# Chunked last stores, a chained transform, epsilon and a middle tap moved between engines

## The chip, the core and the metric

The kernel runs on one core of a Trainium2 chip. Its engines work at the same time, each through its own queue in order: TensorE (PE in the profile, its weight loads PEld) for matrix products into PSUM, VectorE (DVE) and ScalarE (ACT) for elementwise work, GpSimd (POOL) for small arithmetic and for starting transfers, SyncE (SP) only for starting transfers. Sixteen DMA engines move data between HBM and the on-chip SBUF, whichever queue a transfer was started from. The metric is the device time of one execution in microseconds.

## The reference

The input x is 4 batches x 512 times x 128 frequencies x 64 channels in float32; D = 128 x 64 = 8192. Two layers follow each other, all in float32.

Layer 0, per batch:

- attention part: a layer norm over D (epsilon 1e-5), three projections D to 64 (k, v, r), a decayed running sum of k*v over time, times sigmoid(r), projected back to D and added to x;
- frequency convolution: layer norm over D, a 3-tap convolution along frequency that mixes the 64 channels, gelu, added to x;
- time convolution: layer norm over D, then for every one of the D columns its own causal 3-tap filter along time,

```python
xt = jnp.swapaxes(xn, 1, 2)
to = lax.conv_general_dilated(xt, time_W, (1,), [(KS - 1, 0)], ..., feature_group_count=d)
to = to + time_b[None, :, None]
to = layernorm(jnp.swapaxes(to, 1, 2), time_ln_g, time_ln_b)
x = x + to.reshape(b, t, f, h)
```

- feed-forward: 64 to 256, gelu, 256 to 64, added to x.

Layer 1: a moving average over 25 times (ends repeated) is the trend; x minus the trend goes through a real Fourier transform over time, of which 128 modes are kept; each channel's modes are mixed by a complex 128x128 matrix; the inverse transform is added to the trend.

## The kernel before

**Layer 0** holds x column-major: 64 chunks of 128 columns x 512 times per batch, worked on in 32 pairs (tiles of 128x1024). Its stages per batch are project (the projections; J), scan (Z), attend_and_convolve (attention's output and the frequency convolution; A), convolve_time (C), open_feed (O) and feed_forward (F). TensorE's order is written out by hand: `in_turn` runs two generators side by side and takes instructions from each by given shares. The pairs that matter here are C of batch 0 beside A of batch 1, C of 1 beside A of 2, C of 2 beside A of 3, and later C of 3 beside F of 2. The queues of the other engines are ordered by the framework's planner, from its own estimates of durations and from priorities that follow the program; `keep_in_program_order` and `issue_after` tie single instructions.

One step of the time convolution handles one pair of chunks. `normed` loads x2 and normalises it on VectorE (a multiplication at L642 and a subtraction at L645, rows rb and mb broadcast over the pair). `tapped` then, per chunk, takes the last tap and the bias on ScalarE (L650, written to `to`) and adds the middle and first tap with one `scalar_tensor_tensor` each on VectorE (L654, on 511 and 510 elements); GpSimd corrects the first two times (L660) and stores the pair to DRAM (L661). ScalarE squares `to` (L701), and two steps later TensorE adds up sums and squares (`add_up`, L252). For batches 1 and 2, 14 of the 32 pairs are done ahead of time, inside the feed-forward of the batch before (`convolve_ahead`, which calls `tapped` itself); `convolve_time` does the other 18 and squares the 14 that it loads again (buffers with the tag "mid", four of them, which feed_forward uses too). Batches 0 and 3 do all 32 there.

In the same stretch of time, one step of attend_and_convolve costs VectorE three operations on 128x1024: x = a + xp (L540), which frees TensorE's PSUM pair "a", z = x * rb (L544), and, after ScalarE's gelu (L592), x2 = gelu + x (L594), which `add_up` needs.

The four layer norms of each batch end in `rsqrt` (L232): GpSimd adds epsilon (L233) and raises to -1/2 (L234); then TensorE spreads the result over rows (`spread`, L242).

**Layer 1** handles two batches at a time, twice: `transform`, `mix`, `invert`, with 16 slabs of 512 columns per batch. In `transform`, `butterflies` loads two slabs (SP), forms v = first half minus second half and u = their sum for each (L1019), and sum and difference of the two u (ev, L1026); `products` multiplies them (L1041 on v, L1055 on ev, L1064 for the ends) and copies to the spectrum xf. `butterflies` is a generator: the first pair of the second half is drawn piece by piece from within `invert` of the first half. Within one pair the operations are tied one behind the other; from one pair to the next they are not. `mix` goes through 16 groups of four channels: `differ` forms d = real minus imaginary (L1104, VectorE, two buffers), `common` multiplies d (L1110) into one of two PSUM pairs and copies it out on ScalarE (L1116, L1117), `second_turn` copies the remaining part on VectorE (L1152), `own` multiplies the rest (L1123), `join` adds (L1159). `invert` goes through 32 slabs: inverse waves (L1202, L1212), the moving average from the slab's own four chunks of times (L1249) and from halos of 12 neighbouring times (L1256), four additions on VectorE (L1261) and one store of 1 MB by GpSimd (L1264). The last slab of each half takes its four PSUM banks from the two pairs "a", since the next transform's first products take the others.

Of the kernel before, what the change touches and what calls it, by code (L numbers as in the profile page):

```python
# [10 lines left out]
F32 = mybir.dt.float32  # L11
# [69 lines left out]
def layer0(ctx, tc, dram, x, xt, vecs, wkvr, wo, wdec, wconv, fbias, w1, fb1, w2, fb2, x4):  # L81
# [150 lines left out]
    def rsqrt(rs, var):  # L232
        nc.gpsimd.tensor_scalar(rs, var, EPS, None, ALU.add)  # L233
        nc.gpsimd.tensor_tensor(rs, rs, mhalf, ALU.pow)  # L234

# [36 lines left out]
    def moments(mean, square, tag):  # L272

        var, rs, mrs = cols(f"var{tag}"), cols(f"rs{tag}"), cols(f"mrs{tag}")
        nc.vector.tensor_tensor(var, mean, mean, ALU.mult)
        nc.vector.tensor_tensor(var, square, var, ALU.subtract)
        rsqrt(rs, var)
        nc.vector.tensor_tensor(mrs, mean, rs, ALU.mult)
        return rs, mrs
# [146 lines left out]
    def scan(b):  # L426
# [10 lines left out]
        nc.vector.tensor_tensor(sq, sq, mv[:, :, 1], ALU.add)  # L437
        nc.vector.tensor_copy(var, mv[:, :, 1])
        rsqrt(rs, var)
# [206 lines left out]

    def tapped(b, i, xr, to, pinned=False):
        for j in range(2):
            c = slice(2 * i + j, 2 * i + j + 1)
            nc.scalar.activation(  # L650
                to[:, j, :], xr[:, j, :], AF.Identity, bias=tb_all[:, c], scale=vec[:, W2, c]
            )
            for k, w in ((1, W1), (2, W0)):
                tap = nc.vector.scalar_tensor_tensor(  # L654
                    to[:, j, k:], xr[:, j, : SL - k], vec[:, w, c], to[:, j, k:], ALU.mult, ALU.add
                )
                if pinned and j == 0 and k == 1:
                    tc.keep_in_program_order(tap)
        cc = slice(2 * i, 2 * i + 2)
        nc.gpsimd.tensor_tensor(to[:, :, 0:2], to[:, :, 0:2], fix[:, cc, :], ALU.add)  # L660
        nc.gpsimd.dma_start(tod[b][cc].rearrange("c p t -> p c t"), to)  # L661
# [13 lines left out]
    def convolve_time(b):  # L675
# [10 lines left out]
        for k in range(n + 2):  # L686
# [3 lines left out]
            if k < n:  # L690
# [8 lines left out]
                normed(b, made + k, x2, xr, rb, mb, made > 0 and k < 4)  # L699
                tapped(b, made + k, xr, to)  # L700
                nc.scalar.activation(sq, to, AF.Square)  # L701
# [215 lines left out]
def layer1(ctx, tc, x4, wri, dftv, dftu, dftd, dfte, idfte, idfto, avg, avgh, out, after):  # L917
# [36 lines left out]
    def pair():  # L954
        return ps.tile([P, 2, SL], F32, tag="a", name="a", bufs=2)
# [33 lines left out]
    def behind(b, n, ins):  # L989

        return tc.issue_after(ins) if b == 0 and n < 5 else nullcontext()

    def butterflies(b0, n):

# [3 lines left out]
        us, vs, ts = [], [], []  # L998
        made = None
        two = 1 if g == NS // 4 else 2  # L1000
# [5 lines left out]
        for i, xin in enumerate(xins):  # L1006
# [10 lines left out]
            for uv, op in ((v, ALU.subtract), (u, ALU.add)):  # L1017
                with tc.issue_after(made.ins) if made else behind(b, at, after["vector"]):
                    made = nc.vector.tensor_tensor(uv.rearrange("p k n -> p (k n)"), xin[:, 0, :], xin[:, 1, :], op)  # L1019
                if op == ALU.subtract or i == 0:  # L1020
                    yield made
        for op in (ALU.add, ALU.subtract):
            t = io.tile([P, 2, SL], F32, tag="ev", name="ev")
            t_, u0, u1 = (x[:, 0:two, :].rearrange("p k n -> p (k n)") for x in (t, *us))
            with tc.issue_after(made.ins):
                made = nc.vector.tensor_tensor(t_, u0, u1, op)  # L1026
            ts.append(t)
# [56 lines left out]
    def mix(xf, last):  # L1084
# [89 lines left out]
        for g in range(1, NG):  # L1174
# [5 lines left out]
            if g + 2 < NG:  # L1180
                with tc.issue_after(turned[g].ins):
                    differ(g + 2)
# [11 lines left out]
    def invert(b0, xf, ahead):  # L1194
# [33 lines left out]
        def fetch(n):  # L1228
# [11 lines left out]
            blocks[n] = xin, halo, []  # L1240

        def within(n, js):
            xin, _, po = blocks[n]
            if n == G * NS - 1:
                po += [whole[:, k, :] for whole in (pair(), pair()) for k in range(2)]
            for j in js:
                if n < G * NS - 1:
                    po.append(bank())
                nc.tensor.matmul(po[j], lhsT=avg_sb[:, j, :], rhs=xin[:, j, :], start=True, stop=False)  # L1249

        def across(n):
            b, s = divmod(n, NS)
            xin, halo, po = blocks.pop(n)
            for j in range(NT):
                at = slice(32 * j, 32 * j + (HALO if j in (0, NT - 1) else 2 * HALO))
                nc.tensor.matmul(po[j], lhsT=avgh_sb[at, :], rhs=halo[at, :], start=False, stop=True)  # L1256
            pm = halves.pop(n)
            begun = None
            for j in (1, 3, 0, 2):
                with tc.issue_after(begun.ins) if begun else nullcontext():  # L1260
                    nc.vector.tensor_tensor(by_n(xin[:, j, :]), by_n(po[j]), by_c(pm[j % 2][:, j // 2, :]), ALU.add)  # L1261
                if j == 3 and n == G * NS - 1:
                    begun = next(ahead)
            nc.gpsimd.dma_start(  # L1264
                out[b0 + b, :, s * SL : (s + 1) * SL].rearrange("(c p) d -> p c d", p=P), xin
            )

# [17 lines left out]
    with tc.manual_schedule(engines={nc.tensor.engine}):  # L1285
        ahead = butterflies(0, 0)
        for b0 in range(0, B, G):
            xf = spec.tile([P, 2, H, G, NF // 2, 2], F32, tag="xf", name="xf")
            last = transform(b0, xf, ahead)
            ahead = butterflies(b0 + G, 0) if b0 + G < B else iter([None] * 4)  # L1290
            mix(xf, last)
            invert(b0, xf, ahead)
# [105 lines left out]
```

## Time and profile before

| | |
|---|---|
| Median of three runs | 3612.3 us (3609.67 to 3617.32) |
| Profiled execution: time, span | 3609.67 us, 3607.9 us |
| Mean granted TensorE clock | 0.986 |
| Busy: PE, VectorE, ScalarE, GpSimd | 3418.7, 2803.8, 1933.0, 505.1 us |
| DMA | 894 MB, mean 248 GB/s |

The span runs from the first instruction to the last; the time has 1.8 us around it. In the rows of the profile, L12 is line 12 of the kernel before; a row of the timeline gives the start, the time taken, the engine, the line, the output and input tiles, and in brackets the idle time before it with what ended it. Matmuls overlap, so a busy TensorE is not one at its peak. The stages lie roughly so in the span: projection of batch 0 to 245 us, the three pairs C beside A at about 508 to 770, 1190 to 1390 and 1835 to 2020 with feed-forwards between and behind them, layer 1 from 2687, its second half from 3137.

### The profile page before, as it was taken

The numbers are of one execution on the slowest core, as the hardware profiler recorded it, in microseconds if no ns is written. First come the engines' busy times: TensorE is split into PE (matmuls) and PEld (weight loads), VectorE is DVE, ScalarE is ACT, GpSimd is POOL, SyncE is SP. The second block draws the span as 40 slices with busy tenths as digits, with TensorE's granted clock in tenths as the row PEclk, the third lists the DMA queues.
The fourth block names the chain that finished last, engine by engine and source line by source line (L and its number), as shares of the span: only waits on it lengthen the run. The fifth ranks groups of instructions, "written<-read, shape, count | busy, mean of one in ns | idle before, by whom it ended". The sixth has DMA issues, their size and how long they took to land. (4 is left out here: it accounts for less than half of the span.)

```text
span 3607.9 us, 56794 instructions
## 1 busy us (share of the span) xinstructions
PE 3418.7 (95%) x21689; PEld 1279.1 (35%) x21689; DVE 2803.8 (78%) x3524; ACT 1933.0 (54%) x2451; POOL 505.1 (14%) x657
## 2 busy tenths in 40 slices
PE   8999998889998899999999989999999999999998
PEld 3433332234333223443322333334332533325433
DVE  4576779976776896677789799956669788897887
ACT  0023456655666565666656588878877810177200
POOL 0000012210101211011112121110000401004011
PEclk9999999999999999999999999999999999999999
DMA  9886657787885788788568777755659378993687
GB/s 311 294 288 229 219 201 258 253 280 268 285 282 183 252 278 279 271 294 289 180 230 283 238 239 261 247 182 200 221 180 294 102 246 293 309 290 106 230 300 266
DMA packets 410478, 894.00 MB, mean 248 GB/s; under 512 B 31840, under 2 KB 82784, under 8 KB 410208
## 3 DMA queue, kind: packets, MB, share of 16 engines
q1 hardware_dynamic: 336640, 620.46, 52.8%
q0 software_dynamic: 71680, 268.46, 20.5%
q8 instruction: 173, 2.83, 0.3%
q10 hardware_dynamic: 1888, 1.45, 0.1%
q14 instruction: 97, 0.79, 0.1%
HBM read 621.74 MB, written 268.50 MB: 247 GB/s over the span
## 5 line engine op out<-in xcount | busy, mean ns | idle before, releaser
L778 PE MATMUL p<-mid,w_sb 64*64 64x512 f32 x2048 | 550.8, 596 | 17.7 <-DVE wx L791 17.6
L778 PE MATMUL pb<-mid,w_sb 64*64 64x512 f32 x2048 | 533.8, 596 | 0.0
L768 ACT ACTIVATE mid<-m,fb_sb 128x1024 f32<-128x1024 f32 x256 | 284.9, 1113 | 92.1 <-PE m L763 90.9
L768 ACT ACTIVATE mid<-c,fb_sb 128x1024 f32<-128x1024 f32 x256 | 284.6, 1112 | 92.5 <-PE c L763 90.3
L763 PE MATMUL c<-x,w_sb 64*64 64x512 f32 x2016 | 278.4, 606 | 13.0 <-ACT mid L768 6.6
L763 PE MATMUL m<-x,w_sb 64*64 64x512 f32 x2016 | 283.2, 613 | 7.4 <-ACT ob L812 5.4
L1218 ACT COPY two<-a 128x512 f32<-128x512 f32 x64 | 37.5, 586 | 428.2 <-PE a L1202 414.0
L778 PEld LDWEIGHTS p<-mid,w_sb 64*64 64x64 f32 x2048 | 153.9, 135 | 292.7 <-issue 263.1
L413 PE MATMUL a<-xp,wx 128*128 128x512 f32 x512 | 235.2, 603 | 0.5 <-DVE me L269 0.5
L1249 PE MATMUL b<-xin,avg_sb 128*128 128x512 f32 x496 | 223.3, 592 | 0.0
L599 ACT ACTIVATE sq<-x 128x1024 f32<-128x1024 f32 x128 | 135.0, 1055 | 159.4 <-DVE x L594 159.3
L1261 DVE TENSOR_TENSOR xin<-b,pm 128x512 f32<-128x512 f32 x248 | 153.9, 683 | 83.7 <-PE b L1256 73.9
L252 PE MATMUL st<-x,ones 128*32 128x512 f32 x512 | 185.5, 609 | 25.5 <-DVE x L594 25.5
L654 DVE SCALAR_TENSOR_TENSOR to<-kd,vec,to 128x511 f32<-128x511 f32 (+1 forms) x272 | 196.9, 743 | 10.5 <-ACT to L650 8.1
L731 ACT ACTIVATE kd<-kd,vec 128x512 f32<-128x512 f32 x256 | 192.7, 803 | 3.1 <-DVE kd L723 3.1
L540 DVE TENSOR_TENSOR x<-a,xp 128x1024 f32<-128x1024 f32 x128 | 156.1, 1219 | 38.8 <-PE a L536 36.4
L734 DVE TENSOR_TENSOR x<-kd,kx 128x1024 f32<-128x1024 f32 x126 | 154.0, 1222 | 33.5 <-ACT kd L731 33.5
L654 DVE SCALAR_TENSOR_TENSOR z<-x,vec,z 128x511 f32<-128x511 f32 x240 | 175.6, 744 | 5.4 <-ACT z L650 2.3
L791 DVE SCALAR_TENSOR_TENSOR x4t<-p,fb_sb,x 128x512 f32<-128x512 f32 x64 | 47.7, 746 | 159.6 <-PE pb L778 157.1
L536 PE MATMUL a<-rst,wo_sb 64*64 64x512 f32 x1024 | 143.5, 628 | 27.7 <-DVE x L540 25.5
L597 POOL DMA_DIRECT2D x<-x x128 | 93.3, 729 | 531.3 <-DVE x L594 497.2
L722 DVE TENSOR_TENSOR kd<-kh,rm 128x1024 f32<-128x1024 f32 x128 | 155.7, 1219 | 7.1 <-ACT rm L286 4.6
(292 smaller groups left out, 6855.4 us busy)
## 6 DMA issues: line engine op xcount, KB each, us to landing
xp<-in_xt SPq DMA_DIRECT2D x256, 512.0 KB
xin<-x SPq DMA_DIRECT2D x96, 1024.0 KB
kh<-to SPq DMA_DIRECT2D x156, 512.0 KB
x<-x POOLq DMA_DIRECT2D x128, 512.0 KB, 4.3
kx<-x SPq DMA_DIRECT2D x128, 512.0 KB
x<-ob POOLq DMA_DIRECT2D x64, 1024.0 KB, 7.9
out<-xin POOLq DMA_DIRECT2D x64, 1024.0 KB, 7.3
x<-x SPq DMA_DIRECT2D x96, 512.0 KB
```

The source lines that it names most:

```text
L252: nc.tensor.matmul(st[32 * q : 32 * q + 32, :], lhsT=ones, rhs=src[:, j, :], start=first, stop=last,)
L413: nc.tensor.matmul(pa[:, k, :], lhsT=wq[:, j, k * P : (k + 1) * P], rhs=xp[:, j, :], start=first and j == 0, stop=last and j == 1,)
L540: nc.vector.tensor_tensor(x1, at, xp, ALU.add)
L654: tap = nc.vector.scalar_tensor_tensor(to[:, j, k:], xr[:, j, : SL - k], vec[:, w, c], to[:, j, k:], ALU.mult, ALU.add)
L722: nc.vector.tensor_tensor(d, to, pair_of(rb), ALU.mult)
L731: tc.keep_in_program_order(nc.scalar.activation(d[:, j, :], d[:, j, :], AF.Identity, bias=vec[:, B4, c], scale=vec[:, G4, c]))
L734: nc.vector.tensor_tensor(x3, d, x2, ALU.add)
L763: nc.tensor.matmul(pm[halves[j], h, :], lhsT=w1_sb[halves[h], q * H : (q + 1) * H], rhs=x3[halves[h], j, :], start=True, stop=True,)
L768: gelu = nc.scalar.activation(mid, pm, AF.Gelu_apprx_tanh, bias=fb1_sb[:, q : q + 1])
L778: nc.tensor.matmul(sums2[i][j][halves[h], :], lhsT=w2_sb[halves[j], q, :], rhs=mid[halves[j], h, :], start=q == 0, stop=q == 3,)
L1249: nc.tensor.matmul(po[j], lhsT=avg_sb[:, j, :], rhs=xin[:, j, :], start=True, stop=False)
L1261: nc.vector.tensor_tensor(by_n(xin[:, j, :]), by_n(po[j]), by_c(pm[j % 2][:, j // 2, :]), ALU.add)
```

## The change

It has five parts.

1. `rsqrt`: epsilon is no longer added by GpSimd. In `moments` the subtraction that forms the variance becomes one `scalar_tensor_tensor` that adds epsilon too; in `scan` the copy of the variance becomes a `tensor_scalar` that adds it. GpSimd keeps the power.
2. `tapped` takes an optional tile `mid`. With it, ScalarE also multiplies each chunk by the middle tap (two more activations), VectorE's two middle taps are left out, and one VectorE addition over both chunks adds `mid`, shifted by one time, to `to`. `convolve_time` passes such a tile for batches 0, 1 and 2, from the buffers "mid".
3. `butterflies` ties each pair of a transform behind the pair before it on VectorE.
4. In `mix`, d of group 3 is no longer tied behind the first `second_turn`.
5. The last two slabs of the whole kernel are stored by chunks of 256 KB, each behind its own addition, from the SP and ScalarE queues in turn instead of 1 MB from GpSimd. For the very last slab TensorE takes the halo products first and then the own chunks in the order in which the additions follow.

```diff
     def rsqrt(rs, var):
-        nc.gpsimd.tensor_scalar(rs, var, EPS, None, ALU.add)
-        nc.gpsimd.tensor_tensor(rs, rs, mhalf, ALU.pow)
+        nc.gpsimd.tensor_tensor(rs, var, mhalf, ALU.pow)
...
-        nc.vector.tensor_tensor(var, square, var, ALU.subtract)
+        nc.vector.scalar_tensor_tensor(var, square, EPS, var, ALU.add, ALU.subtract)
...
-        nc.vector.tensor_copy(var, mv[:, :, 1])
+        nc.vector.tensor_scalar(var, mv[:, :, 1], EPS, None, ALU.add)
...
+            if mid is not None:
+                nc.scalar.activation(mid[:, j, :], xr[:, j, :], AF.Copy, scale=vec[:, W1, c])
             for k, w in ((1, W1), (2, W0)):
+                if mid is not None and k == 1:
+                    continue
                 tap = nc.vector.scalar_tensor_tensor(
...
+        if mid is not None:
+            nc.vector.tensor_tensor(to[:, :, 1:], to[:, :, 1:], mid[:, :, : SL - 1], ALU.add)
...
-                tapped(b, made + k, xr, to)
+                mid = bk.tile([P, 2, SL], F32, tag="mid", name="mid", bufs=4) if b < B - 1 else None
+                tapped(b, made + k, xr, to, mid=mid)
...
+    behind_pair = [None]
...
-        made = None
+        made = behind_pair[0]
...
-                with tc.issue_after(made.ins) if made else behind(b, at, after["vector"]):
+                with behind(b, at, after["vector"]), tc.issue_after(made.ins) if made else nullcontext():
...
-                made = nc.vector.tensor_tensor(t_, u0, u1, op)
+                made = behind_pair[0] = nc.vector.tensor_tensor(t_, u0, u1, op)
...
-                with tc.issue_after(turned[g].ins):
+                with tc.issue_after(turned[g].ins) if g > 1 else nullcontext():
                     differ(g + 2)
...
+        def final(n):
+            return b0 + G == B and n == G * NS - 1
+
         def within(n, js):
...
+            if final(n):
+                edges(n, True)
+                js = (1, 3, 0, 2)
             for j in js:
...
-                nc.tensor.matmul(po[j], lhsT=avg_sb[:, j, :], rhs=xin[:, j, :], start=True, stop=False)
+                nc.tensor.matmul(po[j], lhsT=avg_sb[:, j, :], rhs=xin[:, j, :], start=not final(n), stop=final(n))
+
+        def edges(n, start):
+            _, halo, po = blocks[n]
+            for j in range(NT):
+                at = slice(32 * j, 32 * j + (HALO if j in (0, NT - 1) else 2 * HALO))
+                nc.tensor.matmul(po[j], lhsT=avgh_sb[at, :], rhs=halo[at, :], start=start, stop=not start)
...
+                if b0 + G == B and n > G * NS - 3:
+                    queue = nc.sync if j % 2 else nc.scalar
+                    queue.dma_start(out[b0 + b, j * P : (j + 1) * P, c], xin[:, j, :])
+            if b0 + G == B and n > G * NS - 3:
+                return
...
             last = transform(b0, xf, ahead)
+            behind_pair[0] = None
```

More of the change, by code (lines that the diff above doesn't have):

```diff
@@ L645, in normed, with tapped @@
         nc.vector.tensor_tensor(xr, xr, pair_of(mb), ALU.subtract)
-    def tapped(b, i, xr, to, pinned=False):
+    def tapped(b, i, xr, to, pinned=False, mid=None):
         for j in range(2):
@@ L1248, in within @@
                     po.append(bank())
-                nc.tensor.matmul(po[j], lhsT=avg_sb[:, j, :], rhs=xin[:, j, :], start=True, stop=False)
+                nc.tensor.matmul(po[j], lhsT=avg_sb[:, j, :], rhs=xin[:, j, :], start=not final(n), stop=final(n))
[4 more added lines that the diff above has]
+                nc.tensor.matmul(po[j], lhsT=avgh_sb[at, :], rhs=halo[at, :], start=start, stop=not start)
         def across(n):
             b, s = divmod(n, NS)
[L1253 to L1256, printed above, removed]
+            c = slice(s * SL, (s + 1) * SL)
+            if not final(n):
+                edges(n, False)
+            xin, _, po = blocks.pop(n)
             pm = halves.pop(n)
@@ L1263, in across @@
                     begun = next(ahead)
-            nc.gpsimd.dma_start(
-                out[b0 + b, :, s * SL : (s + 1) * SL].rearrange("(c p) d -> p c d", p=P), xin
-            )
+                if b0 + G == B and n > G * NS - 3:
[3 more added lines that the diff above has]
+                return
+            nc.gpsimd.dma_start(out[b0 + b, :, c].rearrange("(c p) d -> p c d", p=P), xin)
         fetch(0)
```

## The prediction, made before the changed kernel was run

> **What bounds the kernel now.** I read the page's busy shares first, then the busy time by stretch, then what TensorE waited for, and then the timeline at the places that the change touches.
>
> ```profile
> span 3607.9 us, 56794 instructions
> PE 3418.7 (95%) x21689; PEld 1279.1 (35%) x21689; DVE 2803.8 (78%) x3524; ACT 1933.0 (54%) x2451; POOL 505.1 (14%) x657
> ```
>
> TensorE is the bound over the whole, but a mean hides the stages. The busy time by stretch (length, then busy us of PE, PEld, DVE, ACT, POOL, the clock, DMA share and GB/s):
>
> ```profile
> 545.00:765.00 220.00, 192.58 (x1076) 49.42 (x1076) 218.00 (x242) 133.98 (x184) 59.12 (x80) 0.99 0.78 258
> 1230.00:1400.00 170.00, 158.89 (x1004) 45.14 (x996) 156.01 (x158) 107.53 (x147) 35.64 (x53) 1.00 0.83 282
> ...
> 3152.00:3245.00 93.00, 92.72 (x632) 23.94 (x624) 86.74 (x77) 69.48 (x117) 0.00 (x0) 1.00 1.03 294
> ```
>
> The first stretch is the time convolution of batch 0 beside the attention of batch 1: VectorE is busy 218 of 220 us, TensorE only 88%. There VectorE's work is the time. The second, the same pair of stages for batches 1 and 2, is mixed: TensorE 93%, VectorE 92%. The third is the second transform of layer 1, where the DMA engines are full (1.03). What TensorE waited for, in the rows that the change bears on (total us, times, longest):
>
> ```profile
> PE a L242 <- POOL rs L234: 8.5, 5, 3.4
> PE b L1055 <- DVE ev L1026: 7.0, 3, 5.6
> ...
> PE a L1110 <- DVE d L1104: 5.1, 2, 2.6
> PE p L242 <- POOL rs L234: 4.2, 2, 2.1
> ```
>
> **The middle tap on ScalarE.** Each of 68 steps (32 for batch 0, 18 each for batches 1 and 2, whose other 14 were made ahead by code that passes no mid) loses two VectorE taps and gains one addition over both columns. VectorE's timeline in the first stretch has the price of each, by distance from start to start:
>
> ```profile
> 597.86 1.21 DVE L645 TENSOR_TENSOR kd<-kd,rm 128x1024 f32<-128x1024 f32 x1
> 599.00 1.21 DVE L540 TENSOR_TENSOR x<-a,xp 128x1024 f32<-128x1024 f32 x1
> 600.13 0.73 DVE L654 SCALAR_TENSOR_TENSOR to<-kd,vec,to 128x511 f32<-128x511 f32 x1
> 600.79 1.21 DVE L544 TENSOR_TENSOR z<-x,rm 128x1024 f32<-128x1024 f32 x1
> ```
>
> A tap takes 0.66 us of the engine's time, a two-input operation on 1024 elements 1.13. So a step saves 2 x 0.66 - 1.13 = 0.19 us: 6.1 us in batch 0, 3.4 us each in batches 1 and 2, 12.9 us at most. ScalarE pays two multiplications of 128x512 per step. No row shows exactly this one; it lies between the copy at L1218 without a column operand (0.59 us) and the activation at L650 with two (0.80 us, 0.71 from start to start). I take 0.70, near L650, which reads the same tile. 64 of them are 45 us in batch 0's stage of about 32 x 8.3 = 266 us; ScalarE goes from 61% to 78% there and still has room.
>
> The skill speaks against this edit: the Trainium skill, "ScalarE: Activation LUTs", Rules for kernel authors, wants multiplications on VectorE, not ScalarE. Its timing (What ACT_TABLE_LOAD costs) would give an estimate of 0.71 us for a 512-element activation with one column operand, 1.42 us of ScalarE for 0.19 us of VectorE. By the rule the edit loses; by the rows above it trades idle time for busy time.
>
> In batch 0 I take 5.5 of the 6.1 us: VectorE's list of waits from 560 to 760 is empty, and TensorE needs only 88% of the time. What is queued behind the new wait: the addition needs the second multiplication, and VectorE takes its queue in order, so an addition placed too early holds up the attention's x and z, for which TensorE waits at L536 and L252. In batches 1 and 2 the engines take turns at being late: in 1240 to 1420 VectorE waited 4.3 us in 9 places for ScalarE's to at L650 and 13.3 us for its gelu at L592, both now behind more ScalarE work. I put the two at -0.5 us together, between -6.8 and, if each multiplication delays a gelu by a quarter of itself (36 steps x 2 x 0.18), +13.
>
> **Epsilon on VectorE.** The two VectorE instructions are exchanged for others of the same 128x4 size (0.16 us rows at L275, L276), so they cost nothing new. On GpSimd one instruction goes:
>
> ```profile
> 456.21 0.22 POOL L233 TENSOR_SCALAR rs<-var 128x4 f32<-128x4 f32 x1 [5.93 <-DVE var L276]
> 456.52 1.04 POOL L234 TENSOR_TENSOR rs<-rs,mhalf 128x4 f32<-128x4 f32 x1
> ```
>
> From start to start that is 0.31 us, 16 times. TensorE visibly waited for the result seven times (rows L242 above): 7 x 0.31 = 2.2; I take 2.0, between 0 and 16 x 0.31 = 5.0.
>
> **The transform's order.** In the second transform the next pair's v stands ahead of this pair's last u, and waits for its load:
>
> ```profile
> 3143.81 1.23 DVE L1019 TENSOR_TENSOR v<-xin 128x1024 f32<-128x1024 f32 x1 [2.76 <-DMA xin<-x]
> 3144.95 1.22 DVE L1019 TENSOR_TENSOR u<-xin 128x1024 f32<-128x1024 f32 x1
> 3146.20 2.36 DVE L1026 TENSOR_TENSOR ev<-u 128x1024 f32<-128x1024 f32 x2
> ```
>
> That is the 5.6 us of L1055. Chained, u can follow the additions that end at 3140.97, the first ev is there at about 3143.3, and TensorE goes on 4.1 us earlier. But the next wait stands right behind: the following v at 3150.08 waits 0.26 us for its own load, and from there the DMA engines are full to 3245. The loads set the end; I take 0.3 us, between 0 and 4.1. In the first transform the same hoisting costs TensorE 1.1 us at its start, but VectorE is busy 102.5 of 105 us from 2690 to 2795 with the same work in either order: 0.
>
> **The freed differ.** After the first group of the mix, TensorE stands idle in both halves:
>
> ```profile
> 3276.26 1.01 ACT L1117 COPY other<-a 64x1024 f32<-64x1024 f32 x1
> ...
> 3277.30 1.23 DVE L1152 COPY other<-a 64x1024 f32<-64x1024 f32 x1 [9.45 <-ACT other L1117]
> 3278.56 1.23 DVE L1104 TENSOR_TENSOR d<-xf 128x1024 f32<-128x1024 f32 x1
> ...
> 3280.05 3.59 PE L1110 MATMUL a<-d,w 128*128 128x256 f32 x8 [2.57 <-DVE d L1104]
> ```
>
> VectorE idled 9.45 us before the copy at L1152; without the tie to it the difference d fits in there, once its buffer is free at about 3272. The 2.57 us do not all go: the product needs a PSUM pair that the copy at L1152 frees at 3278.5. What goes is the 1.25 us of d, twice: 2.5 us, between 0 (order unchanged) and 5.1. Beside it, the group of eight took 3.59 us here with a granted clock of 0.50 from 3280.5 to 3283.5, and 1.97 us at full clock in the first half after the same idle time. A shorter idle time may save the 1.6 us; I take half, 0.8.
>
> On that, the Trainium skill, "TensorE: Matmul & The Clock Gate", The HAM clock gate, states that the gate closes after an idle window of about 3.4 us that runs freely. The 2.57 us here already halved the clock once; by the rule that term would be 0, by the row up to 1.6.
>
> **The last slabs.** The end of the trace:
>
> ```profile
> 3597.28 1.14 PE L1256 MATMUL a<-halo,avgh_sb 12*128 12x512 f32 x8
> ...
> 3598.48 2.48 DVE L1261 TENSOR_TENSOR xin<-a,pm 128x512 f32<-128x512 f32 x4 [2.26 <-PE a L1256]
> ...
> 3601.26 0.75 POOL L1264 DMA_DIRECT2D out<-xin  x1 [3.99 <-DVE xin L1261]
> ```
>
> With the halo products first, the own products (0.86 us per chunk) end one after another, and the additions (0.6 us each) keep up: the last ends about 0.7 us after TensorE's 3598.4, at 3599.1 instead of 3600.96, 1.9 us earlier. Then 6.6 us pass today from the issue of 1 MB to the span's end. The last chunk is 256 KB. Rows nearest: 512 KB stores of layer 0 land in 4.0 us (to<-to), 1 MB stores in 5.5 us near the end; the slope gives about 3.2 us. That is 3.4 us less at most; the two slabs' 2 MB, issued from 3594.5 on, need about 6 us at the 350 GB/s of the busiest stretches and would end at the same 3602 to 3603. The new issues stand on SP and ScalarE queues that have nothing left behind them. I take 5.0 us in all, between 2 (only the additions) and 6.
>
> **Sum.** 5.0 + 2.5 + 0.8 + 2.0 + 0.3 + 5.5 + 0.5 = 16.6 us. The profiled execution took 3609.67 us, its span and 1.8 us around it, so it would take 3593.1; the median of the three runs lies 2.6 us above it, and against the median 3612.3 the forecast is 3595.7, rounded to 3596.
>
> **Rivals.** ScalarE gives it back: in all three pairs of stages the later taps and gelus eat VectorE's saving. For it speak the waits for L592 and L650 in batches 1 and 2, against it the empty list of VectorE's waits in batch 0. The C terms become 0 to +4: 3602 to 3606. -- The better case: batches 1 and 2 gain as batch 0 does, for VectorE is at 92% there too: 6.8 instead of 0.5, 3589. -- The change doesn't do what it says: the planner leaves d behind the copy and the chunks end no sooner than the additions (tail 2, mix and clock 0): 16.6 - 6.3 = 10.3, 3602. -- Slower: the addition stands in VectorE's queue ahead of the attention's x while ScalarE is still at the second multiplication. The other parts bring 10.6 us; to end 7.2 us (0.2%, about what a measurement of this kernel can tell from no change) above 3612.3, the steps must lose 17.8 us, 0.26 each, so a wait of 0.45 us per step decides. One whole multiplication laid bare in each step, 0.70 - 0.19, is +35 us: 3637. In batch 0 VectorE has other work between, which speaks against it.
>
> **How the numbers follow.** Forecast 0.50 (own range 3590 to 3602), give-back 0.22, better 0.13, doesn't do what it says 0.07, slower 0.08. Faster by 0.2% means below 3605.1: the first, the better and over half of the give-back, with the best part of the fourth left for no change: 0.76; within 0.2% 0.16; slower 0.08. The low end takes every term near its best (6 + 2.5 + 1.6 + 3 + 1 + 6.1 + 6.8 = 27), 3585; the high end a loss of 10 us in the convolutions against 10.6 gained elsewhere, 3612.
>
> **What would show it.** Right: the stretch of batch 0's convolution about 5 us shorter with VectorE still near 99% and no row of VectorE waiting for ScalarE's mid; L1110's wait for d gone and a wait of 1.3 us for L1152 in its place; L1055's 5.6 us near 1.5 with the transform ending no earlier; the span ending about 4 us after the last L1261 instead of 7. Wrong: VectorE waits at the new addition, longer waits at L594 for L592, or a planner's order elsewhere that moved other work.

## The result, and the profile after

The changed kernel took 3626.6 us (median, 3622.6 to 3635.6) beside 3611.2 us for the kernel before (3609.1 to 3617.3): a ratio of 1.0043, 95% interval 1.0032 to 1.0053. It is 15 us slower, where 16 us faster were forecast.

The head of the page of the changed kernel, the span and the busy shares:

```profile
span 3624.5 us, 56830 instructions
PE 3437.4 (95%) x21689; PEld 1282.6 (35%) x21689; DVE 2793.4 (77%) x3456; ACT 2014.0 (56%) x2587; POOL 514.2 (14%) x639
```

VectorE does 10.4 us less, ScalarE 81 us more, as meant. But TensorE, with the same 21689 matmuls, is busy 18.7 us longer: the loss stands in a row that the change did not touch.

Where it stands shows when the start of TensorE's n-th matmul is compared in both traces (they come in the same stages in the same order). The lag of the changed kernel is -0.1 us at 500 us, ahead of the first time convolution; 0.0 near 1215; **+16.5 us** at the end of batch 1's time convolution beside batch 2's attention and the passage to the next part; and **+30.6 us** after the same pair of stages for batches 2 and 3 (+14.7 there, and -0.7 between). In layer 1 it falls by 9.4 us to the last inverse, and the span, 16.6 us longer, shows that the tail gained 4.6 more. So the four other parts won 14 us here, where 10.6 were forecast for them (part of it by chance, as e13 below shows), and the middle tap lost about 31 us in two stretches where I had put it at half a microsecond of gain. The clock explains little of it: 0.99 was granted to TensorE in the first of the two stretches and 1.00 before, and 0.96 in the second in both kernels.

Busy time by stretch, after, for the first two stretches that the prediction showed (length, PE, PEld, DVE, ACT, POOL, clock, DMA share, GB/s):

```profile
545.00:765.00 220.00, 196.55 (x1078) 50.17 (x1077) 212.97 (x216) 170.32 (x243) 65.52 (x80) 0.98 0.76 263
1230.00:1400.00 170.00, 153.32 (x916) 41.53 (x912) 142.98 (x135) 114.46 (x163) 38.64 (x49) 0.99 0.76 255
```

In the second, VectorE fell from 156 to 143 us and TensorE got 916 matmuls started instead of 1004. An engine that is relieved and does less in the same time, while the bound also does less, is one that waits. What VectorE waited for there, from 1215 to 1470 (total us, times, longest):

```profile
DVE to L657 <- ACT to L649: 10.3, 11, 1.5
DVE to L663 <- ACT mid L653: 10.1, 3, 3.9
```

L663 is the new addition, L653 the new multiplication, L657 the tap that is left, and L649 ScalarE's start of a chunk: the last tap with the bias, which begins `to`. The first of these waits was 4.3 us before (1215 to 1450), the second is new:

```profile
DVE to L654 <- ACT to L650: 4.3, 9, 0.7
```

Beside batch 3's attention (1850 to 2165) it is the same again: 10.8 us at L657, where 3.8 stood before, and 7.0 us in four waits at L663. The timeline of one of the three waits at L663 (start, time taken, engine, line, tiles, in brackets the idle time before and its releaser):

```profile
1307.92 1.06 ACT L714 ACTIVATE sq<-kh 128x1024 f32<-128x1024 f32 x1 [4.03 <-DMA kh<-to]
1308.88 0.71 ACT L653 ACTIVATE mid<-kd,vec 128x512 f32<-128x512 f32 x1
...
1310.92 1.22 DVE L663 TENSOR_TENSOR to<-to,mid 128x1022 f32<-128x1022 f32 x1 [3.86 <-ACT mid L653]
1312.02 1.00 ACT L591 ACTIVATE c<-c 128x1024 f32<-128x1024 f32 x1
...
1314.46 1.22 DVE L593 TENSOR_TENSOR x<-c,x 128x1024 f32<-128x1024 f32 x1
...
1315.73 1.04 PE L251 MATMUL st<-x,ones 128*32 128x512 f32 x2 [2.76 <-DVE x L593]
```

ScalarE stands 4.03 us at L714, the square of a pair that is loaded again from DRAM. The two multiplications of the step are behind it in its queue. VectorE has come to the addition and stands 3.86 us; the gelu (L591) and the attention's sum x2 (L593) come late in turn, and TensorE idles 2.76 us at the reduction that reads x2. The kernel before had the first of these waits too, from 1215 to 1450:

```profile
ACT sq L708 <- DMA kh<-to: 27.5, 10, 3.9
```

There it held up less that VectorE needed at once: none of the waits for ScalarE's start was longer than 0.7 us, and only three waits for a gelu, of 0.8 to 2.6 us, came right behind such a square. This row is one that the prediction did not read.

The other parts, in the list of TensorE's waits over the whole span, after:

```profile
PE st L251 <- DVE x L593: 35.1, 31, 3.5
...
PE st L251 <- ACT sq L598: 9.8, 16, 1.3
PE a L241 <- POOL rs L233: 7.0, 4, 3.1
...
PE a L1118 <- issue: 3.9, 4, 1.2
PE p L241 <- POOL rs L233: 3.5, 2, 1.8
...
PE b L1063 <- DVE ev L1034: 1.8, 1, 1.8
```

The waits for rsqrt went from 8.5 and 4.2 to 7.0 and 3.5 us; the 5.1 us in two waits for the difference d are gone, but the same matmuls (L1118) now stand 3.9 us in four places; the 5.6 us for ev are down to 1.8. The first row, the reduction behind the attention, grew from 25.5 to 35.1, and the second was 1.8 before. And the end:

```profile
3615.79 3.70 PE L1263 MATMUL a<-xin,avg_sb 128*128 128x512 f32 x8
3616.33 4.58 SPq L1286 DMA_DIRECT2D out<-xin  x4
3618.66 2.48 DVE L1281 TENSOR_TENSOR xin<-a,pm 128x512 f32<-128x512 f32 x4 [1.17 <-PE a L1263]
```

The last addition ends at 3621.1, 3.4 us before the span's end; before it was 6.9 us.

### The profile page after: what moved, and what is told of

It is laid out like the page before. It is cut to its first block, busy times and chain, and to the rows that moved or that the text cites. A ratio compares the mean times of both kernels' runs of the same rounds, so it can differ in the third digit from the quotient of the medians.

```text
span 3624.5 us, 56830 instructions
## 1 busy us (share of the span) xinstructions
PE 3437.4 (95%) x21689; PEld 1282.6 (35%) x21689; DVE 2793.4 (77%) x3456; ACT 2014.0 (56%) x2587; POOL 514.2 (14%) x639
## 5 line engine op out<-in xcount | busy, mean ns | idle before, releaser
L251 PE MATMUL st<-x,ones 128*32 128x512 f32 x512 | 195.8, 614 | 35.1 <-DVE x L593 35.1
L539 DVE TENSOR_TENSOR x<-a,xp 128x1024 f32<-128x1024 f32 x128 | 156.3, 1221 | 38.5 <-PE a L535 36.1
L657 DVE SCALAR_TENSOR_TENSOR z<-x,vec,z 128x511 f32<-128x511 f32 x240 | 176.2, 747 | 2.6 <-ACT z L649 1.1
L535 PE MATMUL a<-rst,wo_sb 64*64 64x512 f32 x1024 | 145.6, 636 | 18.1 <-DVE x L539 16.3
L728 DVE TENSOR_TENSOR kd<-kh,rm 128x1024 f32<-128x1024 f32 x128 | 155.8, 1221 | 8.2 <-ACT rm L285 6.3
L1233 DVE TENSOR_TENSOR pm<-even,a 128x512 f32<-128x512 f32 x256 | 158.2, 680 | 2.4 <-PE a L1220 2.3
```

The source lines that it names most:

```text
L251: nc.tensor.matmul(st[32 * q : 32 * q + 32, :], lhsT=ones, rhs=src[:, j, :], start=first, stop=last,)
L539: nc.vector.tensor_tensor(x1, at, xp, ALU.add)
L657: tap = nc.vector.scalar_tensor_tensor(to[:, j, k:], xr[:, j, : SL - k], vec[:, w, c], to[:, j, k:], ALU.mult, ALU.add)
L728: nc.vector.tensor_tensor(d, to, pair_of(rb), ALU.mult)
L1233: nc.vector.tensor_tensor(pm[:, k, :], even[:, i, :], ods[:, i, :], op)
```

## The experiments

Two theories at the start. **A, the order of the queue:** ScalarE's waiting square stands ahead of the multiplications, and VectorE's addition waits behind it. **C, ScalarE's time:** each multiplication adds 0.6 us ahead of gelus, squares and taps, wherever it stands. The multiplications by the middle tap are called products below, whether they are added or not. The table has all runs, with the growth of the two stretches against the trace of before (first: 6000th to 7500th matmul, second: 9900th to 11700th). Two traces of one and the same kernel (e5, e14) differ by 4.2 us in the first stretch, so less than that says nothing there. A ratio is to runs of the kernel before made at the same time on the same chip; the medians of these lie between 3609.1 and 3613.0 us, so two kernels from different groups (e1 to e4, e5 to e8, e9 to e12, e13 to e15) are better compared by their ratios.

| kernel | median us | ratio to before (95%) | first | second |
|---|---|---|---|---|
| changed kernel | 3626.6 | 1.0043 (1.0032 to 1.0053) | 16.5 | 14.7 |
| e1 multiplication alone | 3639.2 | 1.0080 (1.0065 to 1.0096) | 15.6 | 11.5 |
| e2 batch 0 alone multiplied | 3598.9 | 0.9970 (0.9959 to 0.9980) | 0.6 | -2.3 |
| e3 own buffers | 3613.3 | 1.0013 (1.0004 to 1.0022) | 7.2 | 6.8 |
| e4 square of a near pair | 3611.9 | 1.0008 (0.9999 to 1.0018) | 6.8 | 7.4 |
| e5 no multiplication | 3597.0 | 0.9961 (0.9946 to 0.9976) | 0.0 | -0.1 |
| e6 chain alone | 3607.5 | 0.9996 (0.9982 to 1.0009) | 0.1 | -0.1 |
| e7 products unread | 3611.4 | 0.9999 (0.9988 to 1.0011) | 6.7 | 5.4 |
| e8 products written last | 3607.5 | 0.9989 (0.9974 to 1.0005) | 7.1 | 4.4 |
| e9 unread, behind starts | 3600.7 | 0.9973 (0.9962 to 0.9983) | 3.8 | 0.6 |
| e10 read, behind starts | 3606.4 | 1.0000 (0.9990 to 1.0010) | 9.1 | 4.8 |
| e11 unread twice | 3616.6 | 1.0023 (1.0014 to 1.0032) | 10.4 | 7.5 |
| e12 reload ahead | 3601.0 | 0.9975 (0.9966 to 0.9984) | 3.8 | 0.5 |
| e13 no multiplication, no chain | 3598.4 | 0.9975 (0.9967 to 0.9983) | 3.3 | 1.3 |
| e14 as e5, again | 3597.7 | 0.9973 (0.9962 to 0.9983) | 4.2 | 0.3 |
| e15 batch 0, behind starts | 3598.1 | 0.9974 (0.9964 to 0.9984) | 0.2 | 1.0 |

**One part alone, and one batch.** e1 puts `tapped`, with its `mid`, into the kernel before. e2 is the changed kernel with

```diff
-                mid = bk.tile([P, 2, SL], F32, tag="mid", name="mid", bufs=4) if b < B - 1 else None
+                mid = bk.tile([P, 2, SL], F32, tag="mid", name="mid", bufs=4) if b < 1 else None
```

> The kernel before with the middle tap's multiplication on ScalarE for three batches, and nothing else of the change. Theory A (queue order): in batches 1 and 2 ScalarE's queue holds the square of a reloaded pair, which waits 3 to 4 us for its load, ahead of the multiplications, and VectorE's addition waits for them; the lag of the changed kernel grew by 16.5 and 14.6 us in these two stretches, so this kernel should take 3636 to 3644 us. Theory B (the parts act on each other, the multiplication only loses because the transform and the last stores moved): 3605 to 3615 us.

> The changed kernel with the multiplication on ScalarE for batch 0 alone. Theory A: batches 1 and 2 run as before, both losses of 16.5 and 14.6 us go, 3593 to 3598 us. Rival B (the loss is some general delay of ScalarE that batch 0 has as well and only shows later): 3605 us or more. What batch 0 itself is worth: the lag shows 2 us won there and most of it lost at the passage to the next part, so against the same kernel without any multiplication 0 to 2 us.

Both come out as theory A says and not as rival B: 3639.2 us, and 3598.9 us, one above A's range and six below B's. The multiplication alone makes the kernel before 28 us slower; without it in batches 1 and 2 the change is a gain. So the parts need not act on each other to lose this. That batch 0 loses nothing speaks against theory C already, but does not show what ScalarE's time costs in batches 1 and 2.

**The square's place, and its wait.** e3 gives the products buffers of their own; e4 keeps everything and lets the square read a pair that is on chip, so that it computes something else and serves for its time alone:

```diff
-                mid = bk.tile([P, 2, SL], F32, tag="mid", name="mid", bufs=4) if b < B - 1 else None
+                mid = (bk.tile([P, NT, SL], F32, tag="ob", name="mid")[:, 0:2, :] if b < B - 1 else None)
```
```diff
-                    nc.scalar.activation(sq, to, AF.Square)
+                    nc.scalar.activation(sq, xr if mid is not None else to, AF.Square)
```

> The changed kernel with the products in buffers of their own (those of the blocks that the feed-forward stores, idle in these stretches), so that they no longer take the slots of the squares. Theory A1 (the square stands in the queue where it does because products and squares share four slots): the squares may run ahead again, the waits of VectorE's addition fall under a third, 3593 to 3605 us. Theory A2 (the order on ScalarE is set by the work alone, a square still stands ahead of two multiplications in most steps): 3612 to 3626 us.

> The changed kernel in which the square of a reloaded pair is taken of the pair normalized just before, which is on chip, so that ScalarE does the same work but has no load to wait for (in batches 1 and 2 the sums of squares are then of other data; the loads stay, read by TensorE alone). Theory A: the addition no longer waits 3 to 4 us, 3593 to 3602 us. Rival C (the loss is ScalarE's additional 0.7 us per multiplication, in front of gelus and taps): the loss stays, 3618 to 3630 us.

Both landed in the middle, 3613.3 and 3611.9 us: by the medians and the ratios each takes 11 to 15 us of the loss away, and each leaves as much or a little more. So theory A is about half of it: VectorE's addition waits 0.2 us for the products in e3 and not at all in e4, where it waited 10.1 and 7.0 us in the two stretches of the changed kernel. The other half is something else. In e3 (ScalarE, then VectorE, from 1217 to 1460):

```profile
ACT sq L714 <- DMA kh<-to: 27.2, 11, 4.2
ACT mid L653 <- DVE kd L644: 16.5, 9, 3.0
```
```profile
DVE to L657 <- ACT to L649: 12.5, 13, 1.5
```

The square still waits as long as ever, but what stands out now is that ScalarE waits at the multiplication for VectorE's normalized pair (kd), 16.5 us, and VectorE at its tap for ScalarE's start (to), 12.5 us. Each engine stands in its queue waiting for the other. In e4 (VectorE, then ScalarE, from 1221 to 1464) VectorE's wait is much the same, and ScalarE, whose products and squares still share four buffers, waits for VectorE's addition to give them free:

```profile
DVE to L657 <- ACT to L649: 11.0, 12, 1.5
```
```profile
ACT mid L653 <- DVE to L663: 7.0, 4, 2.5
ACT sq L714 <- DVE to L663: 6.3, 6, 1.2
```

So neither variant is free of waits of its own, and both remedies together were not run.

**All without it, and the chain alone.** e5 passes `mid = None`; e6 is the kernel before with the chained butterflies and nothing else.

> The changed kernel with no multiplication on ScalarE at all (last stores, chained transform, freed first differences and epsilon stay). If batch 0's multiplication gains what the forecast gave it (5.5 us), this stands 5.5 us above the variant with batch 0 alone, at 3604 us. If it gains only what the trace showed between two batches' work (1 to 2 us), it stands at 3598 to 3601 us, and the four other parts are worth 11 to 14 us, most of it in the second transform and the tail.

> The kernel before with the second transform's butterflies chained from one pair of blocks to the next, and nothing else. The forecast gave this 0.3 us, since the loads set the pace there; the trace of the changed kernel gained 6.6 us in that stretch. If the chain does it: 3604 to 3606 us and the same 5 to 7 us in that stretch of the trace. If it came from the loads running against other work: within 1 us of before.

e5: 3597.0 us, so the four other parts are worth 10 to 14 us (e5, e14), and batch 0's multiplication (e2: 3598.9) gains nothing. e6 cannot be told from before, though its trace was 7.3 us shorter in the second transform and the mix; e13 below settles this.

**ScalarE's work alone.** In e7 VectorE keeps both taps in batches 1 and 2, and the products, in own buffers, are read by nobody. e9 then ties each behind its own start, which waits for the same input, so that no product stands waiting by itself:

```diff
-            nc.scalar.activation(
+            begun = nc.scalar.activation(
...
-                nc.scalar.activation(mid[:, j, :], xr[:, j, :], AF.Copy, scale=vec[:, W1, c])
+                with tc.issue_after(begun.ins) if b > 0 else nullcontext():
+                    nc.scalar.activation(mid[:, j, :], xr[:, j, :], AF.Copy, scale=vec[:, W1, c])
...
-                if mid is not None and k == 1:
+                if mid is not None and b < 1 and k == 1:
...
-        if mid is not None:
+        if mid is not None and b < 1:
```

> As the variant with buffers of their own, but in batches 1 and 2 VectorE keeps both taps and nobody reads the products, which ScalarE still makes: ScalarE's added work alone, with no addition that waits. Rival C (ScalarE's occupied time delays the gelus and the squares behind which TensorE waits): half of the loss that is left, 7 us in each of the two stretches, stays, 3610 to 3616 us. Theory D (what is left is VectorE standing at the addition, or at the tap whose start ScalarE puts behind two multiplications): under 2 us per stretch, 3597 to 3603 us.

> As the variant with unread products, but in batches 1 and 2 each product stands in ScalarE's queue behind the start of its own half pair, which waits for the same input, so that a product never stands waiting by itself. Theory C1 (ScalarE's added 0.6 us per product delays gelus and squares): still 10 to 12 us above the kernel without products, 3607 to 3612 us. Theory C2 (the products stood waiting for VectorE's normalized pair, 17 us in 8 waits in the first stretch, and held up what was behind them): under 4 us above it, 3597 to 3601 us.

e7 seemed to prove theory C: 3611.4 us, though nobody reads the products. e9 undid that. The same 72 multiplications, 0.61 us each from start to start and so some 44 us of ScalarE's time, cost 3600.7 - 3597.7 = 3 us, which these runs cannot tell from nothing (the ratios of e9 and e14 are both 0.9973). ScalarE had the time to spare; what e7 paid for, 10.7 us by the medians and 9 by the ratios, was the place of the products in the queue. In e7's list (1219 to 1460) they stand waiting, and in e9's (1215 to 1460) no such row is left:

```profile
ACT sq L714 <- DMA kh<-to: 20.0, 10, 3.7
ACT mid L653 <- DVE kd L644: 17.1, 8, 3.4
```
```profile
ACT sq L598 <- DVE x L593: 29.3, 16, 5.7
ACT sq L715 <- DMA kh<-to: 16.8, 7, 3.8
```

**The same remedies with the products read.** e8 writes, with own buffers, both starts ahead of both products; e10 also ties the products behind both starts in batches 1 and 2.

```diff
-            if mid is not None:
-                nc.scalar.activation(mid[:, j, :], xr[:, j, :], AF.Copy, scale=vec[:, W1, c])
...
         if mid is not None:
+            for j in range(2):
+                c = slice(2 * i + j, 2 * i + j + 1)
+                nc.scalar.activation(mid[:, j, :], xr[:, j, :], AF.Copy, scale=vec[:, W1, c])
             nc.vector.tensor_tensor(to[:, :, 1:], to[:, :, 1:], mid[:, :, : SL - 1], ALU.add)
```

> As the variant with buffers of their own, with both starts of a pair written ahead of both products, so that no tap of VectorE waits behind a product where the order is kept. If the wait of the tap for its start (12.5 us in 13 waits in the first of the two stretches, 4.3 in 9 before) makes what is left: 3 to 7 us less than the variant with own buffers, 3606 to 3610 us. If the addition's place or ScalarE's load makes it: 3612 to 3615 us.

> The whole multiplication with addition, own buffers, and in batches 1 and 2 each product behind both starts of its pair in ScalarE's queue. Theory C2: 3597 to 3602 us. Theory C1: no better than the variant with own buffers and both starts written first, 3606 to 3612 us.

e8 came out where it was expected if the tap's wait were the cause, 3607.5 us, but the wait did not go (11.5 us in 11 places): the number fits, the reason is not shown. e10 took ScalarE's wait for kd away and gained nothing over e8: 3606.4 us. VectorE's list in e10 (1215 to 1460), in e9, and without products in e14 (1218 to 1455):

```profile
DVE to L655 <- ACT to L649: 10.3, 10, 1.5
...
DVE to L665 <- ACT mid L664: 3.2, 5, 1.2
```
```profile
DVE to L658 <- ACT to L649: 1.4, 4, 0.5
```
```profile
DVE to L657 <- ACT to L649: 4.6, 9, 0.7
```

Here the kernels differ: at the tap and the addition VectorE waits 13.5 us for ScalarE where the products are read, 1.4 us where they are not, and 4.6 us where there are none; its waits for the gelu are alike (14.2 us in e10, 14.9 in e9). It had 18 x 0.19 = 3.4 us to win in this stretch. Reading the products costs 3606.4 - 3600.7 = 5.7 us by the medians and 10 by the ratios, even in the best order found. That the waits make this is not shown: e10 also has both starts ahead of the products, where e9 has each product behind its own start.

**Twice the products, unread.**

> As the variant with unread products behind their starts, with every product of batches 1 and 2 made twice (ScalarE 2.4 us more per pair and nothing for anyone to wait for). Theory C1: twice that variant's loss over the kernel without products, so 20 us or more, 3617 to 3625 us. Theory C2: about the same as with single products, within 4 us.

3616.6 us, near theory C's range, but not for its reason: a new row of 10.3 us in 8 places shows VectorE waiting at L641 for a buffer kd that ScalarE's second product still reads. It is no clean dose: with this wait in it, it can neither show that the time of the products is free nor that it is not.

**The reloads ahead.**

> The changed kernel without products, with the reloaded pairs asked for two squares ahead, into four buffers instead of two, so that ScalarE's square finds its pair loaded. ScalarE waited 26 us for these loads in the first of the two stretches of the kernel before. If that wait holds up gelus there, 4 to 10 us faster than without it, 3587 to 3593 us; if it is time that ScalarE had to spare, 3595 to 3599 us.

3601.0 us, no gain. But the wait that this was to remove was still 21.9 us in 8 places: two more buffers did not bring the loads forward enough. Inconclusive on what that wait is worth to a kernel without products.

**The chain, and batch 0 once more.** e13 is e5 without the chain, e14 is e5 again on the same chip, e15 multiplies for batch 0 alone, in own buffers and behind both starts.

> The changed kernel without products and without the chain of the transform's butterflies: the last stores, the freed first differences and epsilon alone. In VectorE's order the chain changes one place of each transform, where one subtraction goes before or behind two other instructions, and no other engine's order. If the 6 to 8 us that several traces gained in the second transform come from the chain: 5 us or more slower than the same kernel with it, and a second transform as long as before. If they differ from one execution to the next whatever the order (the multiplication alone, with no chain, gained 2.6 us there; the kernel without products, with it, 3.2): within 2 us of it.

> The changed kernel without products, with the chain, again, on the chip of the run without the chain. Theory chain: 5 us or more faster than without it. Theory execution: within 2 us, and a second transform that differs from that of its first run by some us, though it is the same kernel.

> Products for batch 0 alone, in buffers of their own, each in ScalarE's queue behind both starts of its pair. Batch 0 reloads nothing to square, so nothing there waits for a load; if VectorE's saved time is to pay anywhere it is here: 2 to 5 us faster than the kernel without products. If TensorE's waits only change place there (the wait for the attention's sum shrank by 6 us and those for the reduction and the convolution grew by as much): within 2 us of it.

3598.4, 3597.7 and 3598.1 us: the same. The chain does what it says at one place: from the 18900th matmul, at the end of the first inverse, to the 19000th the kernels with it need 25.1 to 28.0 us, those without it 29.8 to 33.3 (e13, before, e1). But to the 19780th, all but the end of the transform, it took 136.3 us (changed kernel) to 141.9 (e5) with the chain, and 136.9 (e13) to 142.9 (before) without: the early start is lost again by then, and the length differs from execution to execution. The 7 to 9 us that single traces gained in the second transform and the mix are not the chain's: e13 gained 8 there without it.

Batch 0 is where VectorE was at 99%. Without products (e5, 507 to 803), with them (e2, 507 to 802), and with them behind both starts (e15, 512 to 808), the busy times and TensorE's waits were:

```profile
507.00:803.00 296.00, 264.91 (x1467) 75.63 (x1460) 276.46 (x317) 171.98 (x233) 71.64 (x95) 0.99 0.79 266
...
PE st L251 <- DVE x L593: 18.2, 19, 3.6
PE a L535 <- DVE x L539: 7.8, 10, 1.3
...
PE st L251 <- ACT sq L598: 1.5, 5, 0.3
```
```profile
507.00:802.00 295.00, 267.64 (x1457) 76.69 (x1450) 269.13 (x284) 209.97 (x295) 76.87 (x95) 0.98 0.78 265
...
PE st L251 <- DVE x L593: 16.2, 18, 3.5
PE st L251 <- ACT sq L598: 6.2, 9, 1.3
...
PE a L535 <- DVE x L539: 1.7, 4, 0.8
```
```profile
PE st L251 <- DVE x L593: 15.7, 20, 3.3
PE a L535 <- DVE x L539: 4.8, 9, 0.8
PE st L251 <- ACT sq L598: 3.7, 9, 0.6
```

In e2 the wait for VectorE's x at L535 shrank by 6.1 us, and the wait for ScalarE's square of x2 grew by 4.7; in e15 the same rows moved by 3.0 and 2.2, so it is chance that the 6.1 us are just what VectorE saves. In both, all waits together fell by about 3 us and TensorE's busy time rose by about 3 us for the same stages (to 267.6 and, in e15, 268.4 us). The gain was made at one row and lost at the next and in busy time. Part of the busy time can be the clock: 0.98 was granted over the stretch in e2 and e15 and 0.99 in e5, and 0.01 of 296 us is 3 us. What made the busy time grow was not taken apart.

## Why the prediction was wrong

**The step that failed** is "In batches 1 and 2 the engines take turns at being late ... I put the two at -0.5 us together, between -6.8 and ... +13". By the medians of e5, e14 and the changed kernel the multiplication costs 29 us (25 to 30 by the ratios), and by the traces nearly all of it there, about twice the bound of 13. The bound priced a delay of the gelus by ScalarE's added time, and e9 shows that this time costs 3 us or nothing. It left out the order of the two queues: that ScalarE's queue holds an instruction that waits up to 4 us for a load, a row that the trace of before had (27.5 us in the same stretch), and that products and squares take turns in four buffers. About half of the loss goes when one of these two is taken away (e3, e4), and with it VectorE's waits at the addition. Of the other half, the place of the products in ScalarE's queue, where ScalarE stands waiting for VectorE's pair, is shown to cost 9 to 11 us where they are not read (e7 against e9). With the products read, 6 to 10 us stay in the best order found (e10 against e9); the tap's wait for ScalarE's start is the row that differs most, and that it is the cause is argued, not shown.

**The rival "Slower"** had the right place, the addition standing in VectorE's queue ahead of the attention's work, and the wrong cause: not the 0.7 us of a second multiplication, but whatever ScalarE stands waiting for ahead of it. So 0.45 us per step, which was to decide, came from seven waits of 1 to 4 us (10.1 and 7.0 us in all) rather than from each step, and in batches 1 and 2, not in batch 0. I gave it 8%. That is about half of the loss. The later taps of the other half stand in the rival "ScalarE gives it back", at a price of at most 4 us.

**Batch 0's 5.5 us** measured as nothing (e2, e15 against e5, e14). The saving was there: from 508 to 803 VectorE's busy time fell from 275.0 to 269.2 us, 5.8 us where 6.1 were forecast. That it reaches TensorE's end was wrong. VectorE's empty list of waits showed it as the bound of the stretch, but TensorE's list had a second row, for ScalarE's squares (1.5 us), ready to grow.

**The price of a multiplication**, 0.70 us taken, was 0.708 us in the mean over 136. The Trainium skill, "ScalarE: Activation LUTs", Rules for kernel authors, wants multiplications kept off ScalarE. Its verdict held here, though ScalarE's time, which cost 3 us or nothing in e9, was not the reason: as far as the runs show, the reason was the order of two queues.

**What was right, and what was half right.** Epsilon: TensorE's waits for rsqrt shrank by 1.5 and 0.7 us, 2.2 against 2.0. The last slabs: from the 21400th matmul to the span's end 4.4 to 4.7 us less in every trace that has them and 0.0 in the two that have not (e1, e6), against 5.0. The chain: 0.3 us forecast, too little to tell from nothing (e13, e14).

The freed d was mis-sized. In every trace that has it the idle time before the group of eight went from 2.57 to 1.15 or 1.16 us in both halves, 1.4 twice against 1.25 twice, and the group now starts 0.1 us behind the copy that the forecast named. But the next group, which did not wait before, now waits 0.8 to 1.0 us, for its own d comes behind the next copy. So the row went from 5.1 us to the 3.9 us of L1118, 1.2 us against 2.5: here too a gain at one row was partly lost at the next. The clock term is in part luck: the group took 1.97 us in all these traces, so the whole 1.6 us came and not half, but e6, which keeps the wait of 2.56 us, took 1.97 us in both halves as well, so whether there are 1.6 us to win depends on the execution (see the last section).

Together 2.2 + 4.5 + 1.2 + 1.6 = 9.5 us against the forecast's 10.6 without the taps; e5, e13 and e14 are 9 to 14 us faster than before.

**What beats both kernels** is the change without its second part, 0.9961 (0.9946 to 0.9976) and 0.9973 (0.9962 to 0.9983) of before in two runs; the chain can go too (e13, 0.9975).

## What to carry to other kernels

Before work is moved to an engine that has time to spare, list what that engine's queue already waits for: its idle time is not all free, part of it stands in front of something, and a result that another engine needs at once inherits that wait. Splitting one accumulation over two engines can make each wait for the other; here 0.19 us saved per tile did not pay for two such hand-overs. And where the busiest engine is relieved, look for the next row in the list of waits of the engine that sets the time: in batch 0 about 6 us saved on VectorE took some us off one row, put most of them on the next row and on busy time, and took nothing off the end that these runs can tell.

## What the runs showed of the hardware

**Busy time can hide waiting.** TensorE's group of reductions over x2, in the kernel before (1215 to 1435) and after (1215 to 1450):

```profile
L252 PE MATMUL st<-x,ones 128*32 128x512 f32 x112 | 36.8, 600 | 4.3 <-DVE x L594 4.3
```
```profile
L251 PE MATMUL st<-x,ones 128*32 128x512 f32 x112 | 44.8, 610 | 9.6 <-DVE x L593 9.6
```

The same 112 matmuls of the same mean length are busy 8 us longer. 112 x 600 ns are 67 us, so in 36.8 us most of them ran beside one another; each uses 32 columns. The reductions over squares (st<-sq) lie between them in TensorE's order and run beside them too. From the 6000th to the 7500th matmul the time in which a reduction over x2 runs with none over squares beside it grew from 7.6 to 14.7 us, so the lost time is booked as busy. Idle time alone shows 5.3 of this row's 13.3 us. The ends of matmuls in a trace are modelled, so these are not exact.

**The clock.** After 2.56 or 2.57 us of idle time the group of eight took 1.97 us in four of six cases (both halves of the kernel before, of e1 and of e6), and 3.59 and 3.54 us in the second halves of before and e1, at a granted clock of 0.50; after 1.15 to 1.16 us it took 1.96 or 1.97 us in all 28 cases of the other 14 traces. The Trainium skill, "TensorE: Matmul & The Clock Gate", The HAM clock gate, gives the window as about 3.4 us; here a shorter idle time halved the clock twice in six, and none of the short ones did.

**What stays open.** What ScalarE's wait for the reloads, 25.6 us in the first stretch even without products, costs a kernel in which nothing is behind it: e12 did not remove it. What makes the last 6 to 10 us of e10: VectorE's waits at the tap and at the addition were not taken apart, nor the order of starts and products. Whether e3 and e4 together would take the whole loss. And how much of batch 0's added busy time is the clock.
